# A graph layer on one core: more node rows fetched singly by SyncE and ScalarE, with semaphores of their own and byte addresses

## The chip, the core and the metric

The kernel runs on one core of a Trainium2 chip. A core has a tensor engine (TensorE, in the profile PE, its weight loads PEld), a vector engine (VectorE, DVE), a scalar engine (ScalarE, ACT), GpSimd (POOL) and SyncE (SP), which issues transfers. Each engine works through a queue of its own in the order in which the program wrote it; they meet through semaphores. Transfers run on 16 DMA engines that all queues share.

The metric is the device time of one execution in microseconds, as the median of several runs. A profile is one execution that the hardware profiler recorded; its span runs from its first to its last instruction.

## The reference, cut to what matters

12,500 nodes with 64 features, 200,000 edges sorted by their target `dst`; `src` is random.

```python
nodes = node_state[edges].reshape(num_edges, -1)        # x[src], x[dst]
gates = ssp(edge_state @ We1 + be1) @ We2 + be2
soft_cutoff = 1.0 - sigmoid(5.0 * (edges_distance - 3.5))
h = ssp(nodes @ Wn1 + bn1) @ Wn2 + bn2
messages = h * gates * soft_cutoff
message_sum = zeros_like(node_state).at[edges[:, 1]].add(messages)
new_state = node_state + (ssp(message_sum @ Ws1 + bs1) @ Ws2 + bs2)
out = layernorm(x + new_state)                          # ssp(v) = softplus(v) - log 2
```

## The kernel before

**Steps.** The edges are cut into 391 steps of 512 edges, four tiles (k = 0 to 3) of 128 edges each. Step g needs, for each tile, the 128 rows `x[src]` (256 bytes each), laid one on a partition in `xg[:, k, :D]`. Beside them stands a one-hot of 42 columns (`onehot`, VectorE), which says at which of 42 neighbouring nodes of a window the edge ends. `transposes` turns a tile with TensorE, `xcopy` copies it out (ScalarE), `layer1_edge` and `layer1_node` make the first layers, `exps`, `logs` and `softplus` the activation (ScalarE twice, VectorE), `layer2_edge` and `layer2_node` the second layers, `hcut` and `message` the products (VectorE), `scatter` sums the messages in the window with the one-hot, and `window` adds them to `sums` (VectorE).

**The loop.** `for i in range(-3, last - 1)` writes one step's work in an order made by hand: `layer2_edge` of step i - 1, first layer of i + 1, scatter of i - 3, exp and ln of i + 1, transposes of i + 3. Up to `ends` = 380 the first matmul of `layer2_edge` (L293) takes the step's waits in one place: `needs` names the copy and loads of step i + 1 and the gathers and one-hots of step i + 3. After step 380 the order changes and the transposes stay nearer to their use. Finished blocks of nodes are normalized in between (`node_block`).

**How rows arrive.** There are two ways.

- GpSimd gathers a tile by one indirect DMA, its indices from `src_i` (`gather`, L202). This is issued 14 steps ahead (`AHEAD`), and `xg` has 18 buffers.
- 24 of the 1,563 tiles come row by row (`fetch`): each row is a DMA of its own whose address is in a register. `slots_by_rows` puts them at steps 36, 68, ..., 388, tile 3 by SyncE and tile 2 by ScalarE. In every step i each of the two queues loads four row numbers into registers (`values_load...`, a TENSOR_LOAD at L215) and issues four row DMAs (L219); so a tile takes 32 steps. ScalarE issues two between exp and ln and two behind ln, and only in the loop's first branch, up to step 379. That makes 1,520 of its 1,536 rows; the last 16 rows of tile 2 of step 388 are not fetched, and what the buffer held stands in for them.

A row number must become an address: the queue multiplies it by 64 and by 4 (one FUSED_REGOPS), for the rows and likewise for the two window loads of `load`. All these DMAs use the eight semaphore lanes that the framework gives to SyncE's and ScalarE's transfers in turn; each issue waits until the lane's last transfer has landed.

**Loads.** `load(g)` is issued five steps ahead on SyncE: the edge features `eT` (128 KB) and two windows of the node table, `wns` (21 KB each), whose start is loaded into registers for two steps at once (L230, from `base_i`).

**The start.** VectorE reduces `dst_h` to each half step's lowest node (`low`); this goes to memory and back (`low_d`, `base_b`), as do the biases (`pieces`, `row_d`, `rows`), on ScalarE's queue and in this order (L480, L482, L517, L519). Behind them stand ScalarE's copies of the node table (L532). The table is made in 14 pieces (L530, L532, L533, L534). GpSimd gathers the first five steps at once; later ones wait for a VectorE memset of the buffer (L195) that is written between the table's pieces, the first behind the first piece.

Of the kernel before, what the change touches and what calls it, by code (L numbers as in the profile page):

```python
# [42 lines left out]
F32 = mybir.dt.float32  # L43
BF16 = mybir.dt.bfloat16
I32 = mybir.dt.int32
AF = mybir.ActivationFunctionType
OP = mybir.AluOpType
AX = mybir.AxisListType
# [3 lines left out]
SP = mybir.EngineType.SP  # L52
# [4 lines left out]
P = 128  # L57
D = 64
HE = 256
GE = 2 * HE  # L60
W = 42
DW = D + W
PIECES = 3
NB = 512
K = 4
# [8 lines left out]

BLOCK_STEPS = ((2, 3, 4, 4, 6, 7, 8, 9, 10, 14), (2, 3, 3, 4, 5, 6, 7, 8, 9, 10), (1, 2, 1, 2, 3))
ROWS = 4
CUTOFF = 5.0
EPS = 1e-5
LN2 = 0.6931471805599453
# [18 lines left out]
    return steps  # L98


def slots_by_rows(NG):

    return [(g, k) for k in (K - 1, K - 2) for g in range(P // ROWS + 4, NG - 2, P // ROWS)]


@with_exitstack
def gnn_resnorm_kernel(ctx: ExitStack, tc: tile.TileContext, a: dict, out: bass.AP, E: int):
    nc = tc.nc
    x = a["x"]
    N = x.shape[0]  # L110
    NG = a["eT"].shape[1]
    NR = a["dst_h"].shape[1]
    NH = 2 * NG
    NCH = a["xT"].shape[1]
    NBL = -(-N // NB)
    WIDE = max(NBL * NB, N - 1 + W)
    assert NCH * P >= N - 1 + W and NR * P >= NH
    REST = LOADS + 2

    const = ctx.enter_context(tc.tile_pool(name="const", bufs=1))  # L120
    dram = ctx.enter_context(tc.tile_pool(name="dram", bufs=1, space=DRAM))
    loads = ctx.enter_context(tc.tile_pool(name="loads", bufs=LOADS + 2))
# [14 lines left out]
    table = dram.tile([P * NCH, 2 * D], F32, name="table")  # L137
# [1 line left out]
    src_i = const.tile([P, NG, K], I32, name="src_i")  # L139
    rel = const.tile([P, NG, K], F32, name="rel")  # L140
    cut = const.tile([P, NG, K], F32, name="cut")
    base_i = const.tile([1, NR * P], I32, name="base_i")
    far_i = const.tile([1, 1], I32, name="far_i")
    sums = const.tile([P, WIDE], F32, name="sums")

# [8 lines left out]
    ident, least, wn2 = packed["ident"], packed["least"], packed["wn2"]  # L154
# [11 lines left out]
    wns = const.tile([DW, REST, 2, 2 * D], F32, name="wns")  # L166

    xgs, xrs, eTs = {}, {}, {}
    made = {}

    def note(key, ins):
        made.setdefault(key, []).append(ins)
        return ins

    def behind(ins, *keys):

        for key in keys:
            for other in made.get(key, []):
                tc.add_manual_dep(ins.ins, other.ins.name,
                                  mybir.DependencyInfo(mybir.DependencyClass.Sync, mybir.DependencyReason.DATA),  # L180
                                  reason="one place of a step takes its waits")

    by_rows = slots_by_rows(NG)
    rows_i = const.tile([len(by_rows), P], I32, name="rows_i")
    half_of = {nc.sync: 0, nc.scalar: len(by_rows) // 2}

    def padding(g, k):
        return g * GE + k % 2 * HE + k // 2 * P >= E
# [14 lines left out]
                out=xg[:, k, :D], out_offset=None, in_=x,  # L203
                in_offset=bass.IndirectOffsetOnAxis(ap=src_i[:, g, k : k + 1], axis=0)))

    def fetch(i, engine, first=0, count=ROWS):

        n, r = divmod(i * ROWS + first, P)
        if i < 0 or n >= len(by_rows) // 2:
            return  # L210
        n += half_of[engine]
        if r == 0:
            xrs[by_rows[n]] = loads.tile([P, P], F32, name=f"xr{by_rows[n][1]}", bufs=2)
        if first == 0:
            _, row_at[engine] = nc.values_load_multi_w_load_instructions(  # L215
                rows_i[n : n + 1, r : r + ROWS], engines=[engine.engine], min_val=0, max_val=N - 1,
                skip_runtime_bounds_check_because="src holds rows of x")
        for j in range(count):
            note(("gather", by_rows[n][0]), engine.dma_start(xrs[by_rows[n]][r + j : r + j + 1, :D],  # L219
                                                             x[bass.ds(row_at[engine][first + j], 1), :]))  # L220

    row_at = {}
    bases = {}

    def load(g):
        eTs[g] = loads.tile([P, HE], F32, name="eT")
        old = ("scatter", g - LOADS - 2 - 4)
        behind(note(("load", g), nc.sync.dma_start(eTs[g], a["eT"][:, g, :])), old)
        if g % 2 == 0:
            _, at = nc.values_load_multi_w_load_instructions(  # L230
                base_i[0:1, 2 * g : 2 * g + 4], engines=[SP], min_val=0, max_val=N - 1,
                skip_runtime_bounds_check_because="they were clamped to these bounds")
            bases[g], bases[g + 1] = at[:2], at[2:]
        for h in range(2):
            behind(note(("load", g), nc.sync.dma_start(wns[D:DW, g % REST, h, :], table[bass.ds(bases[g][h], W), :])),  # L235
                   old)

    xTs, zs, us, ss, ghs, hs, msgs, scs = ({} for _ in range(8))

    def onehot(g):  # L240
        last = nc.vector.tensor_tensor(xgs[g][:, :, D:DW], iota, rel[:, g, :].to_broadcast([P, K, W]), OP.is_equal)  # L241
        for k in range(K):
            if (g, k) in by_rows:
                last = nc.vector.tensor_copy(xrs[g, k][:, D:DW], xgs[g][:, k, D:DW])
        note(("onehot", g), last)

    def transposes(g):
        tx = tx_tile()[:DW].rearrange("f (k e) -> f k e", k=K)
        for k in range(K):
            row = xrs[g, k][:, :DW] if (g, k) in by_rows else xgs[g][:, k, :DW]  # L250
            nc.tensor.transpose(tx[:, k, :], row, ident)  # L251
        xTs[g] = tx

    def xcopy(g):
        xT = work.tile([DW, K, P], F32, name="xT", bufs=3)
        note(("xcopy", g), nc.scalar.copy(xT, xTs[g]))  # L256
        xTs[g] = xT.rearrange("f (t h) e -> f h t e", h=2)
# [169 lines left out]
    with tc.manual_schedule():  # L427
# [4 lines left out]
        with tc.tile_pool(name="prep", bufs=1) as prep:  # L432
# [11 lines left out]
            for i in range(3):  # L444
                load_x(i)
            nc.sync.dma_start(rows_i, a["rows"])
            dist = cut.rearrange("p g k -> p (g k)")
            nc.sync.dma_start(dist, a["dist_l"])
            dst_i = rel.bitcast(I32)
# [31 lines left out]
            base_b = prep.tile([P, NR * P], F32, name="base_b")  # L481
# [18 lines left out]
            for i, w in enumerate((we2[:D, 0, :], wn2)):  # L500
                n = w.shape[0]
# [16 lines left out]
            rows = prep.tile([PIECES, 4, D], BF16, name="rows")  # L518
# [6 lines left out]
            for i in range(PARTS):  # L525
                for c in range(i * CP, (i + 1) * CP, CP // 2):
                    m = CP // 2
                    ps = z_tile().rearrange("p b (k f) -> p (b k) f", k=K)
                    for k in range(m):
                        nc.tensor.matmul(ps[:, k, :], xT[:, c + k, :], wnb, start=True, stop=True)  # L530
                    tb = prep.tile([P, m, 2 * D], F32, name="tb", bufs=6)
                    nc.scalar.copy(tb[:, :K, :], ps[:, :K, :])  # L532
                    nc.vector.tensor_copy(tb[:, K:, :], ps[:, K:m, :])  # L533
                    nc.sync.dma_start(by_node[:, c : c + m], tb)  # L534
                    nc.vector.memset(sums[:, c * P : WIDE if c + m == NCH else (c + m) * P], 0.0)
                    for g in waiting.get(c // m, []):
                        gather(g, after=True)
                if i == 1:
                    nc.vector.tensor_copy(base_i, base_b[:1])
                    for k in range(2):  # L540
                        nc.vector.tensor_copy(be3[:, k, :], rows[:, 0, :])
                    for k in range(K):
                        nc.vector.tensor_copy(row3[:, :, k, :], rows[:, 1:3, :])
                        nc.vector.tensor_copy(rs3[:, k, :], rows[:, 3, :])
                if i == 2:
                    nc.vector.tensor_scalar(dist, dist, CUTOFF - 1.5, 5.0, OP.subtract, OP.mult)
                    nc.scalar.activation(dist, dist, AF.Sigmoid)
                    nc.scalar.preload_act_table_set("natural_log_exp_and_others")
                    nc.vector.tensor_scalar(dist, dist, -1.0, 1.0, OP.mult, OP.add)
                    nc.vector.tensor_copy(rel, dst_i)  # L550
                    for t in range(2):
                        r = rel[:, :, 2 * t : 2 * t + 2]
                        nc.vector.tensor_sub(r, r, base_b[:, :NH].rearrange("p (g h) -> p g h", h=2))


        with tc.tile_pool(name="finish", bufs=1) as finish:
# [24 lines left out]
            for i in range(-3, last - 1):  # L581
                now = parts.pop(i, [])
                early = [part for part in now if part.tensor]
                at(load, i + LOADS)
                fetch(i, nc.sync)
                if i >= 0:
                    at(gather, i + AHEAD, i < BEHIND)
                if i < ends:
# [11 lines left out]
                    for n, g in enumerate(third[i]):  # L600
                        scatter(g, zs[i + 1][:, 1, HE + 2 * W * n : HE + 2 * W * (n + 1)])
                    at(exps, i + 1)
                    fetch(i, nc.scalar, 0, ROWS // 2)
                    at(logs, i + 1)
                    fetch(i, nc.scalar, ROWS // 2, ROWS // 2)
                    for g in ahead[i]:
                        transposes(g)
                        xcopy(g)
                    for g in second[i]:
                        layer2_node(g)  # L610
                    for g in second[i]:
# [163 lines left out]
def layouts(inputs):  # L775
# [18 lines left out]

    out = {"x": np.ascontiguousarray(x)}
    out["src_l"] = lanes(src, 0)
    out["rows"] = np.ascontiguousarray(out["src_l"].reshape(P, NG, K)[(slice(None), *zip(*slots_by_rows(NG)))].T)
    out["dst_l"] = lanes(dst, dst[-1])
    out["dist_l"] = lanes(dist, 1e6)
    out["dst_h"] = np.ascontiguousarray(padded(dst, NR * P * HE, dst[-1]).reshape(NR, P, HE).transpose(1, 0, 2))  # L800
# [42 lines left out]
```

## Time and profile before

| | |
|---|---|
| runs | 1999.58, 1996.73, 1999.58 us; median 1999.58 |
| profiled execution: its time | 1994.42 us |
| profiled execution: its span | 1992.6 us |
| mean granted TensorE clock | 0.977 |
| GpSimd gathers L202 | 1,539, mean 951 ns |
| single rows | 1,536 by SyncE, 1,520 by ScalarE |
| table pieces to `table` | 14, 448 KB each |

The page's groups give, for each line of the kernel, the engine, the operation, out<-in, how often, the busy us and mean ns, and the idle time just before with what ended it. A "q" behind an engine's name (SPq, ACTq) is its queue issuing something. The order of time has the start in us, the duration in us, engine, line, operation and count, and in brackets the idle time before it. The chain of waits has start, duration and what the time went into. In the table of stretches each engine has its busy us and number of instructions, followed by the granted clock, the DMA engines' busy share and GB/s.

### The profile page before, as it was taken

To read this page: it belongs to the slowest core of one execution; us is meant where nothing else is said; L and a number is where in the kernel's file an instruction comes from. 1 tells how busy PE (TensorE), PEld (TensorE's weight loads), DVE (VectorE), ACT (ScalarE), POOL (GpSimd) and SP (SyncE) were. 2 spreads that over 40 slices of the span, in tenths; PEclk is the share of its full clock that TensorE was granted. 3 is DMA by queue.
4 is the path that set the end of the run, shared out by engine and by line. 5 is a ranking of instruction groups with operands and counts; after the bars stand their busy time and mean duration, and the time that the engine had idled before them with its cause. 6 is when DMAs were issued, how large, how long until landed. Compare 5 with 4: busy or idle time off the path is not lost.

```text
span 1992.6 us, 46151 instructions
## 1 busy us (share of the span) xinstructions
PE 1843.2 (92%) x11373; PEld 1531.6 (77%) x11373; DVE 1082.5 (54%) x2756; ACT 925.0 (46%) x1318; POOL 1463.8 (73%) x1543
## 2 busy tenths in 40 slices
PE   5899999999998998989999899999999999999996
PEld 4788788888777777777777777777887787787775
DVE  4455455555554554645555555555565555555554
ACT  1355455554444444544444444454454444455442
POOL 6777777777777777777777777777777777777770
PEclk9999899999999999999999999999899999999996
DMA  8422222222222222222232222232232222222230
GB/s 239 131 67 70 63 68 70 69 66 69 67 66 65 65 67 63 66 66 63 68 72 62 68 67 68 63 73 63 68 73 68 68 69 68 69 68 68 71 74 10
DMA packets 173687, 143.41 MB, mean 72 GB/s; under 512 B 49324, under 2 KB 145776, under 8 KB 173415
## 3 DMA queue, kind: packets, MB, share of 16 engines
q1 hardware_dynamic: 119758, 87.95, 15.3%
q0 software_dynamic: 49248, 50.53, 13.2%
q10 hardware_dynamic: 4408, 1.90, 0.4%
q8 instruction: 97, 1.59, 0.3%
q14 instruction: 176, 1.43, 0.2%
HBM read 130.57 MB, written 9.63 MB: 70 GB/s over the span
## 4 chain that ended last, share of the span: by engine, by line
PE 73%; SPq 8%; DMA 7%; issue 5%; DVE 2%; ACT 2%; ACTq 1%; POOL 1%; DVEq 0%; POOLq 0%
PE z L268 15%; PE gh L303 11%; PE gh L297 11%; PE z L262 10%; PE z L320 7%; PE tx L251 6%; PE gh L293 6%; DMA xr<-in_x 6%; PE z L260 3%; SPq L235 3%; SPq L219 2%; SPq L215 2%; PE z L530 2%; ACT u L279 2%; DVE h L312 1%
## 5 line engine op out<-in xcount | busy, mean ns | idle before, releaser
L202 POOL DMA_INDIRECT xg<-in_x,src_i x1539 | 1463.6, 951 | 477.8 <-issue 336.7
L279 ACT ACTIVATE u<-z 128x768 f32<-128x768 f32 x392 | 317.4, 810 | 659.1 <-PE z L320 625.3
L312 DVE TENSOR_TENSOR h<-gh,cut 128x256 f32<-128x256 f32 x391 | 166.1, 425 | 686.1 <-PE gh L303 669.8
L282 ACT ACTIVATE u<-u,one 128x768 f32<-128x768 f32 x392 | 365.9, 933 | 304.4 <-DMA xr<-in_x 294.6
L268 PE MATMUL z<-xT,wns 106*128 106x256 f32 x1564 | 415.9, 389 | 0.0
L303 PE MATMUL gh<-consts,s 128*128 128x64 f32 x3128 | 397.8, 271 | 0.0
L303 PEld LDWEIGHTS gh<-consts,s 128*128 128x128 f32 x3128 | 386.5, 194 | 0.0
L287 DVE SCALAR_TENSOR_TENSOR s<-u,z 128x768 f32<-128x768 f32 x392 | 372.8, 951 | 24.3 <-ACT u L282 7.2
L268 PEld LDWEIGHTS z<-xT,wns 106*128 106x128 f32 x1564 | 302.1, 195 | 44.8 <-ACT xT L256 0.7
L297 PE MATMUL gh<-consts,s 128*128 128x128 f32 x1564 | 280.8, 302 | 0.0
L262 PE MATMUL z<-eT,consts 128*128 128x256 f32 x782 | 277.7, 437 | 0.0
L297 PEld LDWEIGHTS gh<-consts,s 128*128 128x128 f32 x1564 | 205.8, 191 | 92.0 <-issue 91.4
L320 PEld LDWEIGHTS z<-xg,msg 128*128 128x128 f32 x1512 | 234.7, 196 | 21.6
L293 PE MATMUL gh<-row,ones 3*128 3x512 bf16 x391 | 148.9, 381 | 103.1 <-DMA xr<-in_x 47.8
L251 PE MATMUL tx<-consts,xg 128*106 128x128 f32 x1540 | 238.0, 278 | 4.0 <-DVE xg L241 2.7
L256 ACT COPY xT<-tx 106x512 f32<-106x512 f32 x391 | 222.4, 569 | 24.4 <-PE tx L251 15.3
L320 PE MATMUL z<-xg,msg 128*128 128x84 f32 x1512 | 221.6, 269 | 0.0
L337 DVE TENSOR_TENSOR sums<-sums,z 64x42 f32 x756 | 148.5, 196 | 129.9 <-issue 116.7
L251 PEld LDWEIGHTS tx<-consts,xg 128*106 128x106 f32 x1540 | 182.9, 144 | 5.2 <-DVE xg L241 3.0
L316 DVE TENSOR_TENSOR msg<-gh,h 128x256 f32<-128x256 f32 x391 | 165.9, 424 | 13.4
L262 PEld LDWEIGHTS z<-eT,consts 128*128 128x128 f32 x782 | 117.7, 190 | 47.6 <-issue 1.5
L293 PEld LDWEIGHTS <-ones 3*128 3x128 bf16 x391 | 35.5, 91 | 140.2 <-issue 122.1
(101 smaller groups left out, 685.5 us busy)
## 6 DMA issues: line engine op xcount, KB each, us to landing
eT<-in_eT SPq DMA_DIRECT2D x391, 128.0 KB
xg<-in_x,src_i POOLq DMA_INDIRECT x1539
xr<-in_x SPq DMA_DIRECT2D x1536, 0.2 KB
xr<-in_x ACTq DMA_DIRECT2D x1520, 0.2 KB
wns<-table SPq DMA_DIRECT2D x782, 21.0 KB
table<-tb SPq DMA_DIRECT2D x14, 448.0 KB
sums<-in_xT SPq DMA_DIRECT2D x7, 455.0 KB
y<-in_x SPq DMA_DIRECT2D x24, 128.0 KB
```

Of the source, the lines that this page charges most:

```text
L202: note(("gather", g), nc.gpsimd.indirect_dma_start(out=xg[:, k, :D], out_offset=None, in_=x, in_offset=bass.IndirectOffsetOnAxis(ap=src_i[ ...
L251: nc.tensor.transpose(tx[:, k, :], row, ident)
L256: note(("xcopy", g), nc.scalar.copy(xT, xTs[g]))
L262: nc.tensor.matmul(zs[g][:, 0, :HE], we1.rearrange("a h d -> a (h d)"), eTs[g], start=False, stop=True, skip_group_check=True)
L268: nc.tensor.matmul(zn, wns[:, g % REST, h, :], xTs[g][:, h], start=True, stop=True, skip_group_check=True)
L279: nc.scalar.activation(us[g][:, part], z_of(g)[:, part], AF.Exp)
L282: nc.scalar.activation(us[g][:, part], us[g][:, part], AF.Ln, bias=one)
L287: nc.vector.scalar_tensor_tensor(ss[g].rearrange("p i t e -> p (i t e)")[:, part], us[g][:, part], BIG, z_of(g)[:, part], OP.min, OP.max)
L293: first = nc.tensor.matmul(gh, ones3[:, :P], row3.rearrange("q i k d -> q (i k d)"), start=True, stop=False, skip_group_check=True)
L297: nc.tensor.matmul(v[:, 0, t], ss[g][:, 0, t, :], we2, start=False, stop=False, skip_group_check=True)
L303: nc.tensor.matmul(ghs[g][:, 1, 2 * t + h, :], ss[g][:, 1 + h, t, :], wn2, start=False, stop=h == 1 and t == 1, skip_group_check=True)
L320: ins = nc.tensor.matmul(sc, msgs[g][:, 2 * t : 2 * t + 2, :].rearrange("p h f -> p (h f)"), xgs[g][:, 2 * t : 2 * t + 2, D:DW], start=t = ...
```

## The change

The rows that come singly get an arrangement of their own.

- `slots_by_rows` now gives 34 tiles, 17 to each queue: tile 3 of steps 28, 50, 71, ..., 370 by SyncE and tile 2 of steps 37, 58, 79, ..., 378 by ScalarE. `pieces_by_row` counts pieces of four rows: SyncE issues two pieces (eight rows) and one in turn, ScalarE one and two, so each 1.5 pieces a step in the mean. A tile's rows are complete `READY` = 8 or 16 steps before its own step. All rows are issued by step 362, 2,176 by each queue; none is left out.
- ScalarE's second piece stands behind the copy of xT.
- Each tile's rows raise a semaphore of their own (four in turn per queue), without waiting for a lane, and the transpose of that tile waits for the full count. The rows are no longer among the `needs` of L293. The tiles lie in four fixed buffers; the first row of a tile waits until the tile before the last has been read.
- Addresses are in bytes: `x` and `table` are viewed as bytes (`U8`), and the row numbers are multiplied beforehand, `rows_i` by 256 in one VectorE instruction at the very start, `base_b` by 512 into a second row of `base_i`. The multiplications in the queues are gone: the built program has 2 FUSED_REGOPS on SyncE instead of 2,320, and none on ScalarE instead of 1,520.
- GpSimd's gathers go from 1,539 to 1,529. VectorE copies the one-hot into a single-row tile 34 times instead of 24.

In the built program the multiplication of `rows_i` is the first instruction of VectorE after the starting barrier and waits for the load of `rows_i`.

```diff
+READY = (8, 16)
+LANDED = 4
+def pieces_by_row(i, queue):
+    return max(0, 3 * i + 3 + (1 - queue)) // 2
 def slots_by_rows(NG):
-    return [(g, k) for k in (K - 1, K - 2) for g in range(P // ROWS + 4, NG - 2, P // ROWS)]
+    slots = []
+    for queue in range(2):
+        n = 0
+        for g in range(READY[queue], NG - 2):
+            if pieces_by_row(g - READY[queue], queue) * ROWS >= (n + 1) * P:
+                slots.append((queue, g, K - 1 - queue))
+                n += 1
+    return slots
...
+    landed = [[tc.alloc_semaphore(f"rows{queue}_{i}") for i in range(LANDED)] for queue in range(2)]
+    x_bytes = x.rearrange("(o n) d -> o (n d)", o=1).bitcast(U8)
+    table_bytes = table.rearrange("(o n) d -> o (n d)", o=1).bitcast(U8)
+    def arrived(g, k):
+        n = by_rows[g, k]
+        queue = slots[n][0]
+        n -= firsts[queue]
+        return landed[queue][n % LANDED], 16 * P * (n // LANDED + 1)
...
-        for j in range(count):
-            note(("gather", by_rows[n][0]), engine.dma_start(xrs[by_rows[n]][r + j : r + j + 1, :D],
-                                                             x[bass.ds(row_at[engine][first + j], 1), :]))
+        for j in range(first, first + count):
+            ins = queues[queue].dma_start(row_tiles[n, "in"][r + j : r + j + 1, :D].bitcast(U8),
+                                          x_bytes[:, bass.ds(row_at[queue][j], 4 * D)])
+            tc.no_tile_sem_insts.add(ins.ins.name)
+            ins.then_inc(arrived(g, k)[0], 16)
+            if r + j == 0:
+                behind(ins, ("rows read", n - 2))
...
-            behind(note(("load", g), nc.sync.dma_start(wns[D:DW, g % REST, h, :], table[bass.ds(bases[g][h], W), :])),
-                   old)
+            behind(note(("load", g), nc.sync.dma_start(
+                wns[D:DW, g % REST, h, :].bitcast(U8),
+                table_bytes[:, bass.ds(bases[g][h], 8 * D * W)].rearrange("o (w f) -> (o w) f", w=W))), old)
...
-            row = xrs[g, k][:, :DW] if (g, k) in by_rows else xgs[g][:, k, :DW]
-            nc.tensor.transpose(tx[:, k, :], row, ident)
+            if (g, k) in by_rows:
+                note(("rows read", by_rows[g, k]), nc.tensor.transpose(tx[:, k, :], xrs[g, k][:, :DW], ident)
+                     .wait_op(*arrived(g, k), "sem-ge"))
+            else:
+                nc.tensor.transpose(tx[:, k, :], xgs[g][:, k, :DW], ident)
...
             nc.sync.dma_start(rows_i, a["rows"])
+            nc.vector.tensor_scalar(rows_i, rows_i, float(4 * D), None, OP.mult)
...
-                    nc.vector.tensor_copy(base_i, base_b[:1])
+                    nc.vector.tensor_copy(base_i[:1], base_b[:1])
+                    nc.vector.tensor_scalar(base_i[32:33], base_b[32:33], float(8 * D), None, OP.mult)
...
                 at(load, i + LOADS)
-                fetch(i, nc.sync)
+                fetch(i, 0, 0)
+                fetch(i, 0, 1)
...
                     at(exps, i + 1)
-                    fetch(i, nc.scalar, 0, ROWS // 2)
+                    fetch(i, 1, 0, 0, ROWS // 2)
                     at(logs, i + 1)
-                    fetch(i, nc.scalar, ROWS // 2, ROWS // 2)
+                    fetch(i, 1, 0, ROWS // 2, ROWS // 2)
                     for g in ahead[i]:
                         transposes(g)
                         xcopy(g)
+                    fetch(i, 1, 1)
```

More of the change, by code (lines that the diff above doesn't have):

```diff
@@ L45 @@
 I32 = mybir.dt.int32
+U8 = mybir.dt.uint8
 AF = mybir.ActivationFunctionType
@@ L116, in gnn_resnorm_kernel @@
     WIDE = max(NBL * NB, N - 1 + W)
-    assert NCH * P >= N - 1 + W and NR * P >= NH
+    assert NCH * P >= N - 1 + W and NR * P >= NH and 8 * D * N < 2**24
     REST = LOADS + 2
+    rows_base = nc.sbuf_base + -nc.sbuf_base % 32
+    nc.alloc_sbuf_tensor("rows", [P, 4 * P], F32)
     const = ctx.enter_context(tc.tile_pool(name="const", bufs=1))
@@ L141, in gnn_resnorm_kernel @@
     cut = const.tile([P, NG, K], F32, name="cut")
-    base_i = const.tile([1, NR * P], I32, name="base_i")
+    base_i = const.tile([33, NR * P], I32, name="base_i")
     far_i = const.tile([1, 1], I32, name="far_i")
@@ L181, in behind @@
                                   reason="one place of a step takes its waits")
-    by_rows = slots_by_rows(NG)
-    rows_i = const.tile([len(by_rows), P], I32, name="rows_i")
-    half_of = {nc.sync: 0, nc.scalar: len(by_rows) // 2}
+    slots = slots_by_rows(NG)
+    by_rows = {(g, k): n for n, (_, g, k) in enumerate(slots)}
+    rows_i = const.tile([len(slots), P], I32, name="rows_i")
+    queues = (nc.sync, nc.scalar)
+    firsts = (0, len([1 for queue, _, _ in slots if queue == 0]), len(slots))
+    landed = [[tc.alloc_semaphore(f"rows{queue}_{i}") for i in range(LANDED)] for queue in range(2)]
[6 more added lines that the diff above has]
+        return landed[queue][n % LANDED], 16 * P * (n // LANDED + 1)
     def padding(g, k):
@@ L204, in gather, with fetch, row_tile @@
                 in_offset=bass.IndirectOffsetOnAxis(ap=src_i[:, g, k : k + 1], axis=0)))
-    def fetch(i, engine, first=0, count=ROWS):
-        n, r = divmod(i * ROWS + first, P)
-        if i < 0 or n >= len(by_rows) // 2:
+    def fetch(i, queue, piece, first=0, count=ROWS):
+        if i < 0 or piece >= pieces_by_row(i, queue) - pieces_by_row(i - 1, queue):
             return
-        n += half_of[engine]
-        if r == 0:
-            xrs[by_rows[n]] = loads.tile([P, P], F32, name=f"xr{by_rows[n][1]}", bufs=2)
+        n, r = divmod((pieces_by_row(i - 1, queue) + piece) * ROWS, P)
+        n += firsts[queue]
+        if n >= firsts[queue + 1]:
+            return
+        _, g, k = slots[n]
         if first == 0:
-            _, row_at[engine] = nc.values_load_multi_w_load_instructions(
-                rows_i[n : n + 1, r : r + ROWS], engines=[engine.engine], min_val=0, max_val=N - 1,
+            _, row_at[queue] = nc.values_load_multi_w_load_instructions(
+                rows_i[n : n + 1, r : r + ROWS], engines=[queues[queue].engine], min_val=0, max_val=4 * D * (N - 1),
                 skip_runtime_bounds_check_because="src holds rows of x")
-        for j in range(count):
-            note(("gather", by_rows[n][0]), engine.dma_start(xrs[by_rows[n]][r + j : r + j + 1, :D],
-                                                             x[bass.ds(row_at[engine][first + j], 1), :]))
-    row_at = {}
+        if (n, "in") not in row_tiles:
+            row_tiles[n, "in"], xrs[g, k] = row_tile(queue, n), row_tile(queue, n)
+        for j in range(first, first + count):
[5 more added lines that the diff above has]
+                behind(ins, ("rows read", n - 2))
+    row_at, row_tiles = {}, {}
+    def row_tile(queue, n):
+        return nc.alloc_sbuf_tensor_at(f"xr{queue}_{n % 2}", [P, P], F32,
+                                       offset=rows_base + (2 * queue + n % 2) * 4 * P).ap()
     bases = {}
@@ L230, in load @@
             _, at = nc.values_load_multi_w_load_instructions(
-                base_i[0:1, 2 * g : 2 * g + 4], engines=[SP], min_val=0, max_val=N - 1,
+                base_i[32:33, 2 * g : 2 * g + 4], engines=[SP], min_val=0, max_val=8 * D * (N - 1),
                 skip_runtime_bounds_check_because="they were clamped to these bounds")
@@ L244, in onehot @@
                 last = nc.vector.tensor_copy(xrs[g, k][:, D:DW], xgs[g][:, k, D:DW])
+                behind(last, ("rows read", by_rows[g, k] - 2))
         note(("onehot", g), last)
@@ L796, in layouts @@
     out["src_l"] = lanes(src, 0)
-    out["rows"] = np.ascontiguousarray(out["src_l"].reshape(P, NG, K)[(slice(None), *zip(*slots_by_rows(NG)))].T)
+    out["rows"] = np.ascontiguousarray(out["src_l"].reshape(P, NG, K)[(slice(None), *list(zip(*slots_by_rows(NG)))[1:])].T)
     out["dst_l"] = lanes(dst, dst[-1])
```

## The prediction

> **What bounds the kernel now.** I read the page's busy table first, then the groups, the table of stretches, and the order of time on the engines that these named.
>
> ```profile
> PE 1843.2 (92%) x11373; PEld 1531.6 (77%) x11373; DVE 1082.5 (54%) x2756; ACT 925.0 (46%) x1318; POOL 1463.8 (73%) x1543
> ...
> L202 POOL DMA_INDIRECT xg<-in_x,src_i x1539 | 1463.6, 951 | 477.8 <-issue 336.7
> ```
>
> PE looks like the bound and POOL like an engine with a quarter of its time free. The second line corrects that: POOL's idle time is mostly "issue", time in which it waits for nothing that is shown. The stretches say the same (columns: length, then busy us and instructions of PE, PEld, DVE, ACT, POOL):
>
> ```profile
> 130.00:200.00 70.00, 70.00 (x451) 58.61 (x451) 39.32 (x97) 35.63 (x48) 52.89 (x57) 1.00 0.28 68
> ...
> 600.00:800.00 200.00, 181.66 (x1147) 150.86 (x1145) 102.59 (x258) 91.10 (x126) 151.48 (x160) 0.99 0.27 66
> ...
> 1000.00:1200.00 200.00, 182.15 (x1163) 151.45 (x1161) 108.15 (x277) 93.89 (x135) 151.34 (x160) 1.00 0.28 68
> ```
>
> POOL issues 160 gathers in every 200 us, 1.25 us each; PE is full at first and at 91% later. In order of time:
>
> ```profile
> 1542.84 1.03 POOL L202 DMA_INDIRECT xg<-in_x,src_i  x1 [0.30 <-DVE s L287]
> 1544.18 0.94 POOL L202 DMA_INDIRECT xg<-in_x,src_i  x1 [0.30 <-PE tx L251]
> ```
> ```profile
> 1540.55 0.37 PE L293 MATMUL gh<-row,ones 3*128 3x512 bf16 x1 [0.36 <-PE gh L303]
> ...
> 1545.84 0.37 PE L293 MATMUL gh<-row,ones 3*128 3x512 bf16 x1 [0.89 <-DMA xr<-in_x]
> ```
>
> POOL's idle 0.30 us stands before every gather, whoever is named as releaser, so a gather costs 0.951 + 0.304 = 1.255 us. L293 waits for the gathers that its loop step transposes. The gather that ended at 1543.87 is the last of those (step 309, for the L293 of step 305), and L293 starts 1.97 us later. I matched all steps this way: from step 90 on the distance has a median of 2.05 us (the landing), although PE can do a step in 4.35 us and did so up to there. Four gathers take 5.02 us. POOL therefore paces PE from step 90 to the gather of step 382, the last that L293 waits for; the last ten steps have gathers in hand.
>
> The start matters too, since POOL stands still in it:
>
> ```profile
> 1.70 8.85 DMA dst_h<-in_dst_h
> 10.57 1.11 DVE dst_h L472
> ...
> 22.52 6.09 DMA row_d<-pieces
> 28.98 1.28 ACT L532
> 30.27 0.59 ACT tb L532
> ```
> ```profile
> 27.75 0.94 POOL L202 DMA_INDIRECT xg<-in_x,src_i  x1 [0.30 <-issue]
> 32.66 0.94 POOL L202 DMA_INDIRECT xg<-in_x,src_i  x1 [3.97 <-DVE xg L195]
> ```
>
> POOL's 21st gather waits for a memset that follows the first table copy on VectorE (L195 behind L533), and that copy hangs on a chain from dst_h's arrival through VectorE to the small loads of row_d and rows. What delays this chain delays POOL, us for us.
>
> **The change part by part.** *Fewer gathers.* Tiles by single rows go from 24 to 34 (17 a queue), POOL's gathers from 1,539 to 1,529. Before step 383 the count matters: 22 of the old tiles (the two of step 388 lie behind) against 34, so 12 gathers less: 12 x 1.255 = 15.1 us off POOL. The two gathers that come back behind step 382 make the last one end at 1941.9 + 2.5 in the old clock; the transposes that read it start at 1963.5, so some 19 us cover them.
>
> *The scaling of rows_i.* The new multiply (rows_i times 256) is the first instruction in VectorE's queue and waits for rows_i's landing; behind it stand the five memsets, L472 and all that follows. Rows_i is issued after three loads of xT. The trace's semaphore records have its data landing between 19.4 and 21.1 us, just behind the third xT load (19.1 to 20.6). It can now be issued at about 4.2 instead of 11.4, but stays behind those loads in its queue, so I keep 20.4. With 0.2 for the multiply and 0.4 for the memsets, L472 starts at 21.0 instead of 10.57: 10.4 us late. Part is absorbed, since low_d and row_d waited in the old run for DMA. VectorE's work from L472 to the last of the pieces ends at 21.35, so now at 31.8; row_d was issued at 22.52 and landed 6.1 us later, behind base_b's 448 KB in ScalarE's queue. Now base_b is issued at about 28 (lowT at 25.1, low_d landing some 3 us later) and lands at about 33.5, and row_d with it at about 34.4, against 28.6. The first table copy, the memset and POOL's 21st gather move by 5.8; 0.5 for the second base_i conversion (an old one takes 0.61 at L539) makes 6.3. Bounds: 4 (row_d lands 1 us after 31.8) and 10.4 (nothing absorbed). The second place where POOL waits for VectorE (2.60 us at 82.33) moves along with the same loop.
>
> [...]
>
> *The SyncE queue.* Per step it issues one eT load (starts 0.412 apart, and 0.047 for a wait), half a base load (0.274), two wns loads and rows. A row costs 0.073 (multiplication, now gone) + 0.060 + 0.279; a load of four addresses 0.65; a wns load 0.075 (gone) + 0.060 + 0.371. New mean with 6 rows and 1.5 address loads: 0.459 + 0.274 + 0.862 + 0.98 + 2.034 = 4.61, with 0.08 for the blocks' y and out 4.69; the old was 4.0 by the same sum. POOL's pace is 1,529 x 1.255 / 391 = 4.91 us a step. SyncE fits by 0.22. In the first steps it can't follow PE's 4.35; that costs nothing while PE has its 52 us in hand (L293 of step 0 at 83.1, its gathers there at 28.7 + 2), which then are used up later than step 90. A byte view of a row is not in the trace: it can cost nothing more than the 0.228 us of the same 256 bytes, or, if the count of elements matters, up to the wns row's 0.320. I take 0.228, the same bytes in the same single run.
>
> *The ScalarE queue.* Before, 0.78 us of idle stood between exp and ln (address load 0.56 and two rows). Without multiplications it becomes about 0.4 (1.25 from exp's start, less 0.81). Every second step adds a load and four rows behind the copy of xT, 0.56 + 4 x 0.32 = 1.84. From exp's start to there it is 2.44 + 1.84 = 4.3 us, inside POOL's 4.91. If that cover were gone, 0.5 us in every second step would show.
>
> *Waits.* Row loads now wait for no semaphore lane (SyncE's queue lost 91.8 + 79.0 us so), and PE waits for rows at the transposes. A tile is complete 8 (SyncE) or 16 (ScalarE) steps before its own step and read 5 or 13 steps later, over 20 us; hidden. VectorE gets ten more copies of 0.2 us at 54% load.
>
> [...]
>
> Sum: 1992.6 - 15.1 + 6.3 = 1983.8 of span. The median of the runs shown is 1999.58, 7.0 over the profiled span (the profiled run itself took 1994.42), so 1990.8.
>
> **Rivals.** (1) The start's delay is hidden: rows_i lands early or the small loads get through faster. For: it is issued 7 us sooner. Against: the xT loads ahead of it. 1999.6 - 15.1 = 1984.5. (2) The delay passes in full: 1999.6 - 15.1 + 10.4 = 1994.9. For: every link is in one queue order; against: row_d's 6.09 us were mostly waiting behind base_b. (3) Slower: SyncE becomes the pace. Place: 355 steps with rows. PE needs 355 x 4.91 - 52 = 1,691 us for them, and the queue may slide from 3 steps ahead to 3.5 behind, 28 us; so it decides from (1,691 + 28) / 355 = 4.84 us a step, is at break-even at 4.87 (0.03 us a row over my price), and at the wns row's price (6 x 0.092 more, 5.24) costs 142 - 9 = 133: 2,133. For: only 0.15 us a step of margin. Against: SyncE's row issues lie between 0.224 and 0.278 us, by one shape. (4) The gathers aren't what L293 waits for; the profile names xr there (47.8 us in 75 waits), PE keeps its pace and the start is made up: no change, 1999.6. Against: the steady 2.05 us behind the gathers. Nothing is added to the last steps: in the built program ScalarE's last row is issued in step 362.
>
> **How the numbers follow.** Forecast 66%, its own range 1987 to 1994 (4 to 10 us of delay, 1 us of noise). Rivals: (1) 9%, (2) 10%, (3) 11%, (4) 4%. A measurement of this kernel tells 0.2%, 4 us, from no change. Faster: 66 + 9 + half of (2) = 80%; within 0.2%: 5 + 4 and a little of (3), 10%; slower 10%. The range takes in (1) and (2) and leaves most of (3) out: 1983.5 to 1996.5.
>
> **What would show it.** POOL's last gather ends near 1935 (1941.9 - 15.1 + 6.3 + 2.5), with 160 in 200 us as before. VectorE's first work after the barrier is the multiply near 20.5; POOL's gap after the 20th gather grows from 4.0 to about 10. SyncE shows no multiplications and rows 0.34 apart; PE's steps are at 4.35 to 4.7 until step 150 or later, then near 4.9. Wrong if POOL shows gaps over 0.30 within the steps, or if L293 stands more than 3 us behind its gathers.

## The result and the profile after

| | before | after |
|---|---|---|
| median, 11 runs each | 1997.22 us (1990.25 to 1999.94) | 1985.48 us (1983.47 to 1992.68) |
| ratio, 95% interval | | 0.9952 (0.9938 to 0.9966) |
| profiled execution: time, span | 1994.42, 1992.6 | 1992.68, 1990.8 |
| GpSimd gathers | 1,539 | 1,529 |
| GpSimd's gap before its 21st gather | 3.97 us | 14.45 us |
| end of the last gather of step 382 | 1905.3 | 1900.4 |
| first matmul of `layer2_edge`, step 378 | 1907.2 | 1902.4 |
| from there to the end of the span | 85.4 | 88.4 |

The kernel is faster by 9.6 us by the ratio (0.48%, interval 6.8 to 12.4; the two medians alone lie 11.7 apart). Step 378's matmul is the one that waits for the last gathers that pace TensorE, so its time separates the paced part of the program from its end. The line numbers have moved: the gather is now L230 (before L202), the first matmul of `layer2_edge` L338 (L293), the cast of `dst_h` L518 (L472), the row DMA L250 (L219), the load of `eT` L268 (L228), the window load L275 (L235). Step 378's matmul before and after, in order of time:

```profile
1907.23 0.37 PE L293 MATMUL gh<-row,ones 3*128 3x512 bf16 x1 [0.22 <-PE gh L303]
```
```profile
1902.39 0.37 PE L338 MATMUL gh<-row,ones 3*128 3x512 bf16 x1 [0.24 <-PE gh L348]
```

The page of the changed kernel, its busy line and three groups:

```profile
PE 1851.2 (93%) x11373; PEld 1538.7 (77%) x11373; DVE 1085.2 (55%) x2768; ACT 922.9 (46%) x1318; POOL 1453.3 (73%) x1533
...
L230 POOL DMA_INDIRECT xg<-in_x,src_i x1529 | 1453.1, 950 | 485.7 <-issue 358.1
...
L327 ACT ACTIVATE u<-u,one 128x768 f32<-128x768 f32 x392 | 366.0, 934 | 237.6 <-ACT u L324 233.0
...
L338 PE MATMUL gh<-row,ones 3*128 3x512 bf16 x391 | 149.5, 382 | 82.6 <-DMA wns<-table 32.9
```

A gather costs what it did (950 ns and about 0.30 of idle). Ten fewer are issued, yet GpSimd's idle time grew by 8 us. ScalarE's idle before ln fell from 294.6 to 233.0 us.

The table of stretches of the changed kernel (length, then busy us and instructions of PE, PEld, DVE, ACT, POOL, then granted clock, DMA share, GB/s):

```profile
130.00:200.00 70.00, 69.18 (x446) 57.99 (x446) 39.23 (x97) 35.50 (x48) 52.91 (x57) 1.00 0.27 66
600.00:800.00 200.00, 188.63 (x1187) 157.16 (x1187) 107.12 (x270) 95.18 (x132) 151.25 (x160) 0.98 0.28 68
1000.00:1200.00 200.00, 192.42 (x1196) 159.60 (x1195) 113.18 (x290) 96.85 (x139) 151.29 (x160) 0.97 0.29 68
```

Again 160 gathers in 200 us: the pace is unchanged, only the count fell. What went the other way is the start. VectorE in order of time, the chain of waits from 0 to 100 us, and GpSimd in order of time:

```profile
20.50 0.22 DVE L492 TENSOR_SCALAR rows_i<-rows_i 34x128 int32<-34x128 int32 x1 [20.50 <-DMA rows_i<-in_rows]
...
20.95 1.08 DVE L518 CAST dst_h<-dst_h 128x1792 f32<-128x1792 int32 x1
```
```profile
4.04 16.44 DMA rows_i<-in_rows
21.02 1.02 DVE dst_h L518
...
31.70 7.84 DMA row_d<-pieces
39.85 1.28 ACT L578
```
```profile
28.14 0.94 POOL L230 DMA_INDIRECT xg<-in_x,src_i  x1 [0.30 <-issue]
43.54 0.94 POOL L230 DMA_INDIRECT xg<-in_x,src_i  x1 [14.45 <-DVE xg L223]
...
93.24 0.94 POOL L230 DMA_INDIRECT xg<-in_x,src_i  x1 [2.64 <-DVE xg L223]
```

VectorE does nothing for 20.5 us. The chain that began with `dst_h`'s arrival now begins with `rows_i`, 17 KB that are issued at 4.04 and land at 20.48, and GpSimd stands still for 10.5 us longer than before. So at step 378 the profile shows 15.1 - 10.5 = 4.6 us of gain where the marks themselves give 4.8; the end then took 3.0 more, and the span gained only 1.8. The eleven runs gained 9.6. The profiled execution was the slowest of them, and the last section shows how an end can differ.

### The profile page after: what moved, and what is told of

It is laid out like the page before. It is cut to its first block, busy times and chain, and to the rows that moved or that the text cites. A ratio compares the mean times of both kernels' runs of the same rounds, so it can differ in the third digit from the quotient of the medians.

```text
span 1990.8 us, 45154 instructions
## 1 busy us (share of the span) xinstructions
PE 1851.2 (93%) x11373; PEld 1538.7 (77%) x11373; DVE 1085.2 (55%) x2768; ACT 922.9 (46%) x1318; POOL 1453.3 (73%) x1533
## 4 chain that ended last, share of the span: by engine, by line
PE 56%; SPq 29%; issue 7%; DMA 3%; DVE 2%; ACT 1%; ACTq 1%; POOL 0%; DVEq 0%; POOLq 0%
SPq L250 11%; PE z L313 11%; PE gh L348 10%; PE gh L342 8%; PE z L307 8%; SPq L275 6%; SPq L244 6%; PE tx L296 5%; PE z L365 5%; PE gh L338 4%; SPq L268 3%; PE z L305 2%; SPq L270 2%; PE z L576 2%; DMA wns<-table 2%
## 5 line engine op out<-in xcount | busy, mean ns | idle before, releaser
L230 POOL DMA_INDIRECT xg<-in_x,src_i x1529 | 1453.1, 950 | 485.7 <-issue 358.1
L327 ACT ACTIVATE u<-u,one 128x768 f32<-128x768 f32 x392 | 366.0, 934 | 237.6 <-ACT u L324 233.0
L332 DVE SCALAR_TENSOR_TENSOR s<-u,z 128x768 f32<-128x768 f32 x392 | 372.7, 951 | 24.4 <-ACT u L327 10.5
L342 PEld LDWEIGHTS gh<-consts,s 128*128 128x128 f32 x1564 | 206.3, 192 | 91.8 <-issue 91.1
L338 PE MATMUL gh<-row,ones 3*128 3x512 bf16 x391 | 149.5, 382 | 82.6 <-DMA wns<-table 32.9
L282 DVE TENSOR_TENSOR xg<-consts,rel 128x168 f32<-128x168 f32 x391 | 128.4, 329 | 0.1
```

The costliest lines, as they stand in the source:

```text
L230: note(("gather", g), nc.gpsimd.indirect_dma_start(out=xg[:, k, :D], out_offset=None, in_=x, in_offset=bass.IndirectOffsetOnAxis(ap=src_i[ ...
L327: nc.scalar.activation(us[g][:, part], us[g][:, part], AF.Ln, bias=one)
L332: nc.vector.scalar_tensor_tensor(ss[g].rearrange("p i t e -> p (i t e)")[:, part], us[g][:, part], BIG, z_of(g)[:, part], OP.min, OP.max)
L338: first = nc.tensor.matmul(gh, ones3[:, :P], row3.rearrange("q i k d -> q (i k d)"), start=True, stop=False, skip_group_check=True)
L342: nc.tensor.matmul(v[:, 0, t], ss[g][:, 0, t, :], we2, start=False, stop=False, skip_group_check=True)
```

## The experiments

The two theories of the start: A, what delays the chain delays GpSimd and with it step 378 us for us (some 10 us in the changed kernel); B, part of it is absorbed and 6.3 pass, as predicted.

**The multiply taken out of the way.** The changed kernel with the multiply of `rows_i` behind the fourth of the table's 14 pieces (`i == 1`):

```diff
             nc.sync.dma_start(rows_i, a["rows"])
-            nc.vector.tensor_scalar(rows_i, rows_i, float(4 * D), None, OP.mult)
...
                 if i == 1:
+                    nc.vector.tensor_scalar(rows_i, rows_i, float(4 * D), None, OP.mult)
                     nc.vector.tensor_copy(base_i[:1], base_b[:1])
```

> The changed kernel with the multiplication of rows_i moved from the start of VectorE's queue to the place of base_i's conversion (behind two table pieces). Theory A (GpSimd's start is delayed us for us; in the profile of the changed kernel its gap before the 21st gather is 14.45 us instead of 3.97): the gap goes back to about 4, the last gather ends about 10.5 earlier (1928.8 instead of 1939.3), and the time falls by about 10 us, a ratio to the kernel before of about 0.990. Theory B (most of the delay is absorbed, the prediction's 6.3): gap 4, but only 6 us less, 0.992. Theory C (the start is made up later, SyncE is the pace): no change, 0.995.

GpSimd in order of time:

```profile
27.88 0.94 POOL L230 DMA_INDIRECT xg<-in_x,src_i  x1 [0.30 <-issue]
33.66 0.94 POOL L230 DMA_INDIRECT xg<-in_x,src_i  x1 [4.83 <-DVE xg L223]
```

Median 1978.22 us, ratio to the kernel before 0.9919 (0.9893 to 0.9945). The gap is 9.6 us shorter than in the changed kernel and step 378 comes at 1890.2, 12.2 us earlier. By the profile that is A. By the ratios to before it is 0.0033, 6.6 us, with intervals that overlap: the times alone allow either.

**The multiply put into the kernel before.** Here by 1.0, so that it changes nothing but the queue:

```diff
             nc.sync.dma_start(rows_i, a["rows"])
+            nc.vector.tensor_scalar(rows_i, rows_i, 1.0, None, OP.mult)
```

> The kernel before with one instruction added: rows_i times 1 at the start of VectorE's queue. Theory A: GpSimd's gap before its 21st gather grows from 3.97 to about 14, and the time by about 10 us, ratio 1.005. Theory B: gap about 10, 6 us, 1.003. Theory C: 1.000.

```profile
29.06 0.95 POOL L202 DMA_INDIRECT xg<-in_x,src_i  x1 [0.30 <-issue]
43.31 0.94 POOL L202 DMA_INDIRECT xg<-in_x,src_i  x1 [13.31 <-DVE xg L195]
```

GpSimd's gap grew by 9.3 us, step 378 moved by 11.4 (1918.6), and the ratio is 1.0052 (1.0032 to 1.0071), 10.4 us. Profile and times agree: the delay passes nearly whole. B's 6.3 lies just outside this interval (6.4 to 14.2).

**The load first.** The changed kernel with the load of `rows_i` ahead of everything, the multiply still first on VectorE:

```diff
         with tc.tile_pool(name="prep", bufs=1) as prep:
+            nc.sync.dma_start(rows_i, a["rows"])
...
-            nc.sync.dma_start(rows_i, a["rows"])
             nc.vector.tensor_scalar(rows_i, rows_i, float(4 * D), None, OP.mult)
```

> The changed kernel with the load of rows_i put before dst_h's and xT's loads; the multiplication stays first on VectorE. Rows_i lands by about 5 us, before dst_h (8 to 10.5), so by theory A VectorE starts its chain at 10.6 as before, the gap is about 4 and the ratio about 0.990; by C 0.995. If the delay was not the wait for rows_i but the multiplication's place in itself, it stays at 14 us of gap.

```profile
28.34 0.94 POOL L230 DMA_INDIRECT xg<-in_x,src_i  x1 [0.31 <-issue]
34.55 0.94 POOL L230 DMA_INDIRECT xg<-in_x,src_i  x1 [5.26 <-DVE xg L223]
```

The gap is 5.26 us, step 378 at 1891.9, ratio 0.9931 (0.9907 to 0.9954). So it is the wait for the landing behind the `xT` loads, not the instruction: moved ahead of them, the same multiply leaves the gap within 0.5 us of the late multiply's. This rests on the profile. The ratio was expected near 0.990, and its interval overlaps that of the changed kernel (0.9938 to 0.9966).

**No wait for the table at all.** The late multiply, and the gathers of steps 5 to 17 no longer behind memsets:

```diff
-FREE = 5
+FREE = 14
...
-                    at(gather, i + AHEAD, i < BEHIND)
+                    at(gather, i + AHEAD)
```

> As the first of these (multiplication late), and GpSimd's first 18 steps of gathers wait for no memset (all of the first 14 steps are issued at the start). The two gaps of 4.0 and 2.6 us go. By A another 4 to 6 us less, ratio about 0.9875, as long as GpSimd doesn't run into the 18 buffers of xg (step 18's gather needs the scatter of step 0, near 95 us, which costs it about 2 of the 6.6). If the early gathers slow the loads of the start, PE's first step is later, which PE's reserve of 50 us should hide. By C no difference to the first.

GpSimd shows neither gap, and step 378 comes at 1885.7, 4.5 us earlier than with the late multiply alone, of the 6.9 us that the two gaps had beyond the usual 0.30; where the other 2.4 us went is not shown. Median 1968.39, ratio 0.9859 (0.9822 to 0.9895): faster than both kernels, by 28 us than the one before.

**One piece a step.** The late multiply, and four rows a step on each queue instead of six, with everything else of the change kept: 22 tiles and 1,541 gathers.

```diff
-    return max(0, 3 * i + 3 + (1 - queue)) // 2
+    return max(0, i + 1)
```

> The kernel of e1 (multiplication late) with one piece of four rows a step on either queue: 22 tiles by rows instead of 34, 1,541 gathers, the own semaphores and byte addresses kept. Theory A (a gather costs GpSimd's pace 1.255 us, and GpSimd sets the end): 12 gathers more, 15 us more than e1, GpSimd's last gather near 1942.5 instead of 1927.5, ratio to before about 0.9995. Rival (the gain came from the semaphores and addresses, as PE no longer waits for rows): as e1, 0.992.

Step 378's matmul with the late multiply, and here:

```profile
1890.18 0.37 PE L338 MATMUL gh<-row,ones 3*128 3x512 bf16 x1
```
```profile
1910.11 0.39 PE L338 MATMUL gh<-row,ones 3*128 3x512 bf16 x1
```

The last gather of step 382 ends at 1907.6 against 1888.4 with the late multiply, 19.2 us later; step 378 19.9 later; ratio 1.0006 (0.9984 to 1.0029), 17 us more. The 12 gathers account for 15; the rest is a mean distance of gathers of 1.2547 us against 1.2520 over some 1,440 of them behind the start, and why it differs is not shown. With semaphores, byte addresses and all, but with the old number of rows, the kernel is no faster than before: the gain is that of the gathers, and the cheaper rows only make room for them.

**Row numbers instead of byte addresses.** The rows are addressed by number, `rows_i` is not multiplied beforehand, and each row's multiplication is back in its queue:

```diff
-            ins = queues[queue].dma_start(row_tiles[n, "in"][r + j : r + j + 1, :D].bitcast(U8),
-                                          x_bytes[:, bass.ds(row_at[queue][j], 4 * D)])
+            ins = queues[queue].dma_start(row_tiles[n, "in"][r + j : r + j + 1, :D],
+                                          x[bass.ds(row_at[queue][j], 1), :])
```

> The kernel of e1 with row numbers instead of byte addresses for the single rows (the two multiplications stand in the queues again, one FUSED_REGOPS a row; the windows keep byte addresses). SyncE needs 6 x 0.073 = 0.44 us a step more. In e1 PE follows SyncE at a mean of 4.82 us a step from step 100 to 350 and GpSimd's reserve is nearly used up there (2.7 us at step 350), so hardly anything covers it: 355 x 0.44 = 156 us more than e1, some 2,130 us (SyncE theory). By the prediction's own sum (4.69 + 0.44 = 5.13 against a limit of 4.84): 103 us more, 2,080. If GpSimd alone sets the end: no change.

Two executions, 2150.18 and 2150.41 us, ratio 1.0771 (1.0723 to 1.0820). The stretches, and what GpSimd waited for:

```profile
600.00:800.00 200.00, 179.51 (x1069) 149.10 (x1068) 98.17 (x250) 86.20 (x123) 137.03 (x147) 0.93 0.26 60
1000.00:1200.00 200.00, 184.14 (x1092) 152.43 (x1091) 102.01 (x259) 88.71 (x129) 140.68 (x150) 0.93 0.27 62
```
```profile
POOL xg L230 <- issue: 380.0, 1245, 0.6
POOL xg L230 <- PE z L365: 156.4, 106, 5.8
```

147 and 150 gathers in 200 us instead of 160: GpSimd no longer sets the pace, it waits 156 us for TensorE to give back buffers, and TensorE follows SyncE at 5.26 us a step over steps 60 to 220 (4.77 with the late multiply): of each two steps the nearer L338 starts 1.7 us (median) behind SyncE's issue of its windows. The third rival of the prediction (SyncE as the pace) is what a dearer row would have brought, here 172 us more than with the late multiply.

**More rows for ScalarE, with and without relief for SyncE.** Both start from the kernel without memset waits. In the first ScalarE issues two pieces a step (40 tiles, 1,523 gathers), in the second SyncE also goes back to one (34 tiles, 1,529 gathers as in the change):

```diff
-    return max(0, 3 * i + 3 + (1 - queue)) // 2
+    return max(0, 2 * i + 2 if queue else (3 * i + 4) // 2)     # first
+    return max(0, 2 * i + 2 if queue else i + 1)                # second
```

> The kernel of e4 (no memsets) with two pieces a step on ScalarE instead of 1.5: 40 tiles, 1,523 gathers, 39 of the tiles before step 383. If GpSimd sets the end: 5 x 1.255 = 6.3 us less than e4, about 0.9827. If SyncE's pace (unchanged) sets it: less gain, 0 to 4 us, with L338 1.5 to 2 us behind the issue of the windows up to the last steps. If ScalarE, at eight rows in every step (4.6 us between its exps in the profile of the changed kernel), becomes the pace: slower than e4.

> The kernel of e4 with one piece a step on SyncE and two on ScalarE: 34 tiles as in the changed kernel (33 before step 383), so GpSimd's work is that of e4 but for one gather (+1.3 us). SyncE falls to about 3.6 us a step. If SyncE's pace in the first 250 steps is covered by GpSimd's reserve, as the prediction has it, the time stays that of e4 plus 1.3 us, while PE's steps between 100 and 200 fall from 4.8 to 4.35-4.6 us and PE meets GpSimd sooner. If SyncE's pace costs time: faster than e4.

The first: GpSimd ends the gathers of step 382 at 1875.3, 8.2 us earlier, but step 378 follows at 1883.7, only 2.0 earlier; median 1971.27, ratio 0.9876 (0.9839 to 0.9913), no gain that can be told. L338 stands 8.4 us behind its gathers there. From step 60 to 350, of each two steps the nearer one starts 1.9 us (median) behind SyncE's issue of its windows: with six gathers less, SyncE is the next bound. ScalarE, whose eight rows a step are the rival, is not: with the same rows on it the second kernel goes through steps 20 to 90 at 4.44 us a step, the first at 4.71. The second: median 1973.96, ratio 0.9896 (0.9859 to 0.9933), step 378 at 1889.2, 3.5 later. GpSimd's gathers of step 382 end 3.7 later: one gather more is 1.3 of it, and their mean distance is 1.2544 us against 1.2529. TensorE now meets GpSimd at about step 100 to 125, not 230 as in the changed kernel, and gains nothing by arriving there sooner; from then on its steps take GpSimd's 4.88 us, not the 4.35 to 4.6 expected between steps 100 and 200. The engines' shares of the chain that ended last, of the changed kernel and of the second:

```profile
PE 56%; SPq 29%; issue 7%; DMA 3%; DVE 2%; ACT 1%; ACTq 1%; POOL 0%; DVEq 0%; POOLq 0%
```
```profile
PE 80%; DMA 5%; issue 4%; DVE 4%; ACTq 3%; ACT 2%; POOL 2%; DVEq 0%; SPq 0%; POOLq 0%
```

The chain of the changed kernel gives SyncE's queue 29% (8% before) and GpSimd nothing. Taking SyncE out of the chain altogether bought nothing, and the 12 gathers put back on GpSimd cost 17 to 20 us. Two queues run here at nearly one pace, and the chain names the one that came last by a hair.

## Why the prediction was right, and where a term was off

- *Fewer gathers, 15.1 us: right.* 160 gathers in 200 us before and after; the 12 gathers cost 17 to 20 us when put back. What GpSimd's busy share hides, its idle 0.30 us before every gather, is what the whole sum stands on.
- *The start's delay, 6.3 us (4 to 10.4): right in its cause and its first links, too small in the profile.* The links up to `row_d`'s issue came as worked out: `rows_i` landed at 20.48 (20.4), L518 began at 20.95 (21.0), `base_b` was issued at 27.40 (28), `row_d` at 31.70 (31.8). The step that failed is "row_d with it at about 34.4": it landed at 39.54, and `base_b`, put at 33.5, had its last increment at 39.95. The prediction put only `base_b` ahead of `row_d`. But SyncE's four `xT` loads, issued behind `row_d` in the kernel before (from 22.92 against 22.52), are now ahead of it (from 26.64 against 31.70):

```profile
22.92 6.73 SPq L442 DMA_DIRECT2D sums<-in_xT  x4
```
```profile
26.64 1.59 SPq L487 DMA_DIRECT2D sums<-in_xT  x4
```

  These are 1.82 MB, with `base_b` 2.27 MB, and from 26.64 to 39.54 that is 176 GB/s; the page's first slice, 50 us long, shows 206 GB/s. That the queues' load is what held `row_d` is argued from this order; that the delay passes nearly whole is shown by the second experiment, where `row_d` took 7.93 us in the same place (chain of waits):

```profile
31.39 7.93 DMA row_d<-pieces
```

  The absorption was counted from a link that the delay itself made worse. How large the delay is in the mean run of the changed kernel stays open: its profile says 10.5, its runs (15.1 - 9.6 = 5.5) would fit 6.3. The runs fall in two groups, though: three before at 1990.25 to 1992.60 and eight at 1996.73 to 1999.94, nine after at 1983.47 to 1988.61 and two at 1992.50 and 1992.68. Group by group the means differ by 5.9 us, nearer to the 4.8 at step 378; the rest of the 9.6 would then be how many runs fell in which group. That is argued, since the groups show in the times alone.
- *SyncE hidden: right, with hardly any margin.* A row was issued in 0.228 us as before, 0.322 apart in the median (0.34), so the byte view costs nothing. SyncE in order of time:

```profile
700.01 0.37 SPq L268 DMA_DIRECT2D eT<-in_eT  x1
700.48 0.78 SPq L275 DMA_DIRECT2D wns<-table  x2
701.99 3.18 SPq L250 DMA_DIRECT2D xr<-in_x  x8
705.26 0.37 SPq L268 DMA_DIRECT2D eT<-in_eT  x1
706.29 0.77 SPq L275 DMA_DIRECT2D wns<-table  x2
707.78 1.24 SPq L250 DMA_DIRECT2D xr<-in_x  x4
709.12 0.37 SPq L268 DMA_DIRECT2D eT<-in_eT  x1
```

  A step of eight rows takes 5.25 us and one of four 3.86, 4.55 in the mean (4.61). Over steps 60 to 220, with its waits, TensorE follows SyncE at 4.75 us a step, against the limit of 4.84: the margin was 0.09, not 0.15 to 0.22. GpSimd's reserve (from the end of a step's gathers to the L338 that waits for them) is 64 us at step 0, 18.5 at step 100, 7 at step 200, and at the landing's 2 us at about step 230 ("150 or later"). So up to there SyncE sets TensorE's pace, and the sign "L293 stands more than 3 us behind its gathers" would have called the prediction wrong; the reserve that its own sum counts covers this. From step 240 to 378 the median is 2.26 us. The multiplications, 2,176 of them on each queue, are together worth 172 us.
- *ScalarE hidden: right; its price was not.* Idle before ln is 233.0 us in 358 times, 0.65 us instead of 0.4: the first row behind an address load took 0.455 us in the median (0.540 at most), the others 0.223. From exp to exp an eight-row step is 4.59 us, inside the pace, and with two pieces in every step (the last experiment) TensorE still made steps of 4.44 us from step 20 to 90, where GpSimd had a reserve.
- *Waits of rows: hidden.* On SyncE the loads of `eT` and of rows no longer wait for a lane that a row holds (91.8 and 79.0 us before). The landing of `rows_i` shows as two increments of its semaphore, at 20.22 and 20.48 (before: twelve, 19.44 to 21.11). In the second experiment 24 rows, issued in the same place (4.07 us), had the last of twelve increments at 20.14, 0.3 us sooner; with one execution of each, what the ten rows more cost stays open.
- *GpSimd's end:* "near 1935" was 1939.3, the 4.2 us of the start.
- *The number:* 1985.48 for 1990.8. The before runs' median moved from 1999.58 (three) to 1997.22 (eleven), and the predicted ratio, 0.9956, stands beside 0.9952 measured. That they are so near is in part luck: at step 378 the profile shows 4.8 us of gain where the sum has 15.1 - 6.3 = 8.8. The rivals: the hidden delay fell with the profile's gap; SyncE as the pace held for the first 230 steps at no cost and set the time only where rows cost more; L293 not waiting for gathers fell with the kernel of one piece a step; "the delay passes in full" is what the profiled execution shows, 6.3 is what the runs still allow.

## What to carry to other kernels

An engine that idles a fixed 0.3 us before every instruction can be full, whatever its busy share and the chain of waits say (GpSimd before: 73% busy, 1% of the chain); count its instructions per stretch, and test it by giving it a few more or less. A preparatory instruction goes behind the chain that others wait for, or its load goes to the front: one multiply of 0.22 us, queued first, cost about 10 us of 15 gained (10.5 in the profile, 10.4 in the runs of the second experiment). When a chain is delayed, list again what is issued ahead of each of its loads, since others that were behind may have passed, as the four `xT` loads did here (first one at 26.64, `row_d` at 31.70).

## What the hardware did that was not expected

The granted clock falls to one half for the last part of every profiled execution, and for how long differs: 35.1 us before, 38.9 after, 16.5 with the late multiply, 16.8 in the last experiment and 35.4 to 39.2 in the others. Stretches of the changed kernel, and of that last experiment:

```profile
1955.00:1965.00 10.00, 10.00 (x35) 7.80 (x36) 3.18 (x8) 2.33 (x3) 0.00 (x0) 0.50 0.05 15
1965.00:1975.00 10.00, 9.23 (x37) 7.36 (x35) 3.69 (x11) 2.91 (x7) 0.00 (x0) 0.50 0.00 0
```
```profile
1940.00:1952.00 12.00, 10.98 (x70) 8.46 (x70) 6.87 (x19) 5.24 (x10) 0.00 (x0) 1.00 0.04 13
```

From step 378 to the end of the span, the executions with 35 us or more at half clock took 85.4 to 88.8 us, and the two with 16.5 and 16.8 took 80.8 and 78.1. Runs of one kernel lie up to 13 us apart (1987.53 to 2000.92 for the kernel before, beside the later experiments), with the late multiply in two groups (1972.88 to 1974.26 and 1982.17 to 1983.04), which the end would explain; that is argued, since only profiled executions show when the clock is low, and the mean clocks of the runs (0.970 to 0.976 in the first group, 0.959 to 0.974 in the second) don't part the groups. It is also why single spans say less here than the time of step 378.

Ahead of that last part the clock falls to one half for shorter stretches and comes back after each: in the changed kernel 13 times for 3.4 us, three times for 6.8 and once for 13.7. In the last part it does not: from 1955 to 1975 us in the rows above TensorE is busy for 19.2 of 20 us at 0.50, and the clock stays there to the end of the span. What makes it fall or come back is not shown.
